# A two-layer vision kernel: the last token groups' routing moved among the second attention's first steps

## The chip, the cores and the metric

The kernel runs on one core of a Trainium2 chip, as one launch. The metric is device time in microseconds. Three runs of the kernel before took 2015.39, 2020.72 and 2024.27 us; the median is 2020.72. A separate execution was profiled; all rows below come from it.

## The reference

The input x is 2 images of 256 channels and 56 x 56 pixels, in float32. Layer 0 normalises groups of channels, makes q, k and v by a 1x1 and a depthwise 3x3 convolution, and lets each pixel attend to a 7x7 neighbourhood: four heads with dilation 1 (branch 0), four with dilation 2 (branch 1). The projected result is added to x. Layer 1 sees the 6272 pixels as tokens of 256 values: a linear attention (one sum of keys and values per image) with a feed-forward part, then a mixture of experts. Cut to what matters here:

```python
x = x + _L0_conv_ref(_gn(x), ...)                 # convolutions, 7x7 neighbourhood attention
t = _to_tokens(x)
t = t + _L1_attn_ref(_ln_t(t), ...)               # linear attention and feed-forward
t = t + _L1_ffn_ref(_ln_t(t), ...)                # 8 experts, the best 2 of each token
# in _L1_ffn_ref
logits = xt @ Wr + br
top_p, top_idx = jax.lax.top_k(softmax(logits), 2)
weights = top_p / top_p.sum(axis=-1, keepdims=True)
h = gelu(einsum('end,edh->enh', layernorm(xt) * ln_g + ln_b, W1) + b1)
y = einsum('enh,ehd->end', h, W2) + b2
```

All of it has to be computed, and the output has the shape of x.

## The kernel before

The program is written as Python generators that are stepped in turn, and a planner (a list scheduler in the compiler) orders each engine's instructions from it. Inside a block marked as a manual schedule, TensorE keeps the order of the program text. The other engines and the DMA queues take the planner's order, which is fixed at compile time; each queue works strictly in order on the chip. Buffers are tiles in pools. A pool that opens on bytes of closed pools makes each of its tiles wait for the last users of the tiles that lay there.

The work runs in these stages. First, image 0: convolutions and neighbourhood attention together (`first_image`). Second, `layer1` begins with image 0's half of the linear layer (`linear`, half 0) while the convolutions of image 1 end. Third, the neighbourhood attention of image 1 (`Attention`, b = 1), with expert tiles of image 0's tokens filled in between its steps. Fourth, image 1's half of the linear layer, also mixed with expert tiles. Last, the rest of the expert tiles and the output.

In half 0 the tokens go in six groups of 512 (four blocks of 128), by `steps` and a table of letters, `parts`: each letter advances one generator by one step. `q` and `m` are queries and messages, `f` is `feed_forward` (four products with a ReLU, `oc` 0 to 3, then the output products two blocks at a time), `r` and `p` are both `route`. `route` has these steps: in the first, TensorE multiplies the router's weights with the tokens (`pa`), an engine copies the product to `la`, VectorE takes the tokens' statistics, GpSimd two powers, and VectorE writes normalised tokens to `row`. In the second, TensorE turns `la` (`pl`), and VectorE finds the best two experts (`top_two`) and counts (`cnt`). In the third, TensorE gives each token its rank among its expert's (`pp`), VectorE makes the indices `si`, and the ACT queue stores the tokens to y2 (`store`). Then come four steps of two scatters each: GpSimd's queue writes 128 rows to `xs` at the indices (L166).

After the last group, `Experts` opens its pools, loads small constants and makes from the counts a table of 17 expert tiles (`full_tiles`, product `pc`, L1356, some 20 small VectorE operations). An expert tile (`Experts.run`) is fetched (`fetch`: rows `xr` from `xs`, weights `w1e` and `w2e`, 1 MB each, all on SP's queue; `so` and `sv`, L1525 and L1529, pick the expert's scales and biases), turned (`turn`, L1538), and multiplied by W1 (L1569) and W2 (L1587), and its result is scattered to y2.

The second attention then opens its own pools. Band by band (8 rows of keys in branch 0), `prepare(g)` loads a group of 448 tokens' q and k in two tiles `ld` (L779, two buffers in all), and four parts of it turn them on TensorE (L747) and copy them out (L756 to L764 and the helper at L180 and L182). `table` loads a band's bias table in eight DMAs (L690, `tab`; in branch 0 two buffers). A score step multiplies keys and queries (L637), takes the exponential on ScalarE (L641), multiplies by the table on VectorE (L642), and multiplies by the values `v` (L651); VectorE adds the result to strips (L815) that GpSimd has cleared (L823). `wpr` holds the projection's weights (L616). Each step of the attention yields; from step 22 on (`LEAD`) one step of the expert tiles follows most of them, and the first expert step is the first tile's `fetch`.

Of the kernel before, what the change touches and what calls it, by code (L numbers as in the profile page):

```python
# [20 lines left out]
P = 128  # L21
# [42 lines left out]
LEAD = 22  # L64
XW = C + 4
# [59 lines left out]
def hybrid_kernel(ctx: ExitStack, tc: tile.TileContext, a: dict, out: bass.AP):  # L125
# [471 lines left out]
    class Attention:  # L597
# [6 lines left out]
        def __init__(self, ctx, b, order, banks=None):  # L604
            self.b, self.banks = b, banks
            kw = {"reuse_waits": "tile"} if banks else {}
            self.pool = {
                k: ctx.enter_context(tc.tile_pool(name=f"p2{k}{b}", bufs=self.POOLS[k], **kw)) for k in order.split()
            }
            self.ps_o = ctx.enter_context(tc.tile_pool(name=f"p2po{b}", bufs=1, space=PSUM, **kw))  # L610
            if banks:
                banks.open(ctx)
            self.ps_s = ctx.enter_context(tc.tile_pool(name=f"p2ps{b}", bufs=1, space=PSUM, **kw))
            bp, op = self.pool["b"], self.pool["x"]
            self.wpr = op.tile([P, 2, C], F32, name="wpr", bufs=1)
            nc.sync.dma_start(self.wpr, a["w_proj_t"].rearrange("(s p) o -> p s o", p=P))  # L616
            self.ones = op.tile([TT, HD], F32, name="ones2", bufs=1)
            nc.vector.memset(self.ones, 1.0)
            self.qT0 = bp.tile([P, HH, WW], F32, name="qT0")

            self.qT1 = bp.tile([P, 2, 2, 28, 28], F32, name="qT1")
            self.kT1 = bp.tile([P, 2, 2, 2, 28, KC], F32, name="kT1")
            self.o0 = op.tile([P, HH, WW], F32, name="o0", bufs=1)
            self.held = {}
# [51 lines left out]
        def table(self, s, r, c):  # L676

            held = self.held
            if held.get(s, (None, None))[0] != r:
                nr, (i0, ni), nw = KR[s], rows_of[s][r], wide[s]  # L680
                t = self.pool["t"].tile(
                    [TT, NH * (KR[s] + 6) * nw], F32, name=f"tab{s}", bufs=2 if self.banks and s == 0 else 1
                )
                t = t[: nr * KC, : NH * ni * nw].rearrange("p (h i j) -> p h i j", h=NH, j=nw)
                urgent = tc.high_priority if self.banks and r == 0 and s == 0 else nullcontext
                for kr in range(nr):

                    f = fp[s][1 if r == 0 and kr < 7 else 2 if r == 2 and kr >= nr - 7 else 0]
                    with urgent():
                        ld = nc.sync.dma_start(  # L690
                            t[kr * KC : (kr + 1) * KC].rearrange("p h i j -> p h (i j)"),
                            bass.AP(
                                f.tensor, f.offset + (i0 + 7 - kr) * nw,
                                [[NH * 21 * nw, KC], [21 * nw, NH], [1, ni * nw]],
                            ),
                        )
                held[s] = (r, t)
                anchors["table"] = ld.ins
            if c is None:
                return held[s][1]  # L700
            o = sum(n for _, n in cols_of[s][:c])
            return held[s][1][:, :, :, o : o + cols_of[s][c][1]]

        def run(self):
# [69 lines left out]
            def prepare(g):  # L774

                lds = []
                for k in range(2):
                    ld = ldp.tile([P, 2, 2 * C], F32, name="ld")[:TT]
                    nc.sync.dma_start(ld, yqk[:, 4 * g + 2 * k : 4 * g + 2 * k + 2, :])  # L779
                    lds.append(ld)  # L780
                if banks is None:
                    pm = ps_s.tile([P, 4, 512], F32, name="s_ps")
                    for k in range(4):
                        turned(lds, k, pm[:, k, :])
                    for k in range(4):
                        settle(g, k, pm[:, k, :])
                    return []

                def part(k):
                    pm = banks()  # L790
                    turned(lds, k, pm)
                    settle(g, k, pm)

                return [(g, lambda k=k: part(k)) for k in range(4)]
# [15 lines left out]
            def blocks(rows):  # L810

                return -(-min(rows, HH) * WW * 3 * C // (T * P))
# [7 lines left out]
            def strip0(j):  # L820
                if j not in strips0:
                    strips0[j] = ac.tile([P, 2, 8, WW], F32, name="acc0")
                    nc.gpsimd.memset(strips0[j], 0.0)  # L823
                return strips0[j]

            def band0(r):
                yield blocks(8 * r + 16)
                yield from prepared(r + 1, 1)
# [103 lines left out]
            def band1(r):  # L932
                if r == 3:
                    anchors["last"] = True
                yield blocks(14 * r + 20)
# [381 lines left out]
    class Experts:  # L1317
# [4 lines left out]
        def __init__(self, ctx, tk):  # L1322
# [4 lines left out]
            self.wp, self.w, self.small = pool("p4w", 1), pool("p4w1", 2), pool("p4s", 2)  # L1327
# [168 lines left out]
        def fetch(self, t, nh, pools):  # L1496
# [28 lines left out]
            nc.gpsimd.tensor_tensor(  # L1525
# [83 lines left out]
    def linear(ph, tk, half, behind=None):  # L1609
# [67 lines left out]
        nc.gpsimd.memset(ones, 1.0)  # L1677

# [198 lines left out]
        def feed_forward(n0, n, m2T, out):  # L1877
# [3 lines left out]
            for oc in range(4):  # L1881
                p1 = ps_h.tile([P, 512], F32, name="p1", tag="h")
# [9 lines left out]
            out.append(lb)  # L1892
# [38 lines left out]
        def top_two(lg, up, lb, scale, row, n):  # L1931


            p = sm.tile([P, 4, E], F32, name="prob")[:, :n]
            iob = iota.unsqueeze(1).to_broadcast([P, n, E])
            nc.vector.tensor_tensor(p, lg, bc(up, E), ALU.mult)
            nc.vector.tensor_tensor(p, p, lb[:, :n], ALU.add)
            nc.vector.tensor_tensor(p, p, bc(scale, E), ALU.mult)
            nc.vector.tensor_tensor(p, p, brb.unsqueeze(1).to_broadcast([P, n, E]), ALU.add)
# [16 lines left out]
        def weights(ms, row, n):  # L1956

            r = sm.tile([P, 4], F32, name="rsum")[:, :n]
# [8 lines left out]
        def route(n0, n, lb):  # L1967

            xT = tk.turned(n0, n)
            pa = ps_a.tile([P, 512], F32, name="pa", tag="a")  # L1970
            for ct in range(2):
                for k in range(n):
                    nc.tensor.matmul(
                        pa[32 * k : 32 * k + 32, :P], wr[:, ct, :], xT[:, ct, k * P : (k + 1) * P],
                        start=(ct == 0), stop=(ct == 1), skip_group_check=True,
                    )
            la = lp.tile([P, P], F32, name="la", bufs=1)
            evac(la[: 32 * n, :], pa[: 32 * n, :P])
# [13 lines left out]
            up = sm.tile([P, 4], F32, name="up1")[:, :n]  # L1992
            nc.vector.tensor_scalar(up, tk.up[:, n0 : n0 + n], 1.0, None, ALU.add)
            if n == 4:
                row = lp.tile([P, 4, XW], F32, name="row")
            else:
                row = wk.tile([P, 2, XW], F32, name="row2", tag="z")[:, :n]
            for k in range(n):
                last = norm(row[:, k, 0:C], t[:, k, :], mv, rs, k)
            with tc.issue_after(last.ins):  # L2000
# [3 lines left out]
            pl = ps_a.tile([P, 4, 32], F32, name="pl", tag="a")  # L2004
            nc.tensor.transpose(
                pl.rearrange("p k e -> p (k e)")[:, : 32 * n], la[: 32 * n, :], ident[: 32 * n, : 32 * n]
            )
            ohs, ms = top_two(pl[:, :n, :E], up, lb, r1, row, n)
# [8 lines left out]
            weights(ms, row, n)  # L2017
            yield
            pp = ps_a.tile([P, 4, E], F32, name="pp", tag="a")
            nc.tensor.matmul(pp[:, :n], tri, m[:, :n], start=True, stop=False)  # L2020
            nc.tensor.matmul(pp[:, :n], ones, before[:, :n], start=False, stop=True)
            slot = sm.tile([P, 4, E], F32, name="slot")[:, :n]
            nc.vector.tensor_tensor(slot, pp[:, :n], ebase.unsqueeze(1).to_broadcast([P, n, E]), ALU.add)
# [53 lines left out]
        def keep():  # L2077
# [8 lines left out]
            wk=wk, ps_h=ps_h, ps_q=ps_q, ps_a=ps_a, ps_k=ps_k,  # L2086
# [23 lines left out]
    def layer1(whole, tk, conv_ctx=None, conv=None, behind=None):  # L2110
# [14 lines left out]
        with ExitStack() as ph:  # L2125
            ln = linear(ph, tk, 0, behind)
            with tc.manual_schedule(engines={mybir.EngineType.PE}):
                for i, _ in enumerate(ln.keys()):
# [9 lines left out]
                    "mfpPPPPfmfrfrff", "fpPPPPffrffrf", "pPPPPrr", "pPPPP",  # L2138
                )
                todo = steps(ln, order[:early1], parts, {"k": conv, "w": merging, "x": prepared})  # L2140
                for part in islice(todo, sum(len(t) for t in parts[:8])):
                    pass
# [5 lines left out]
            for _ in islice(todo, len(parts[8])):  # L2148
                pass
            ex = Experts(whole, tk)  # L2150
            table = ex.full_tiles(ln.ps_a.tile([P, E], F32, name="pc", tag="a"), ln.ones)
            next(table)
            for _ in todo:
                pass
            for _ in table:
                pass

        xc = whole.enter_context(tc.tile_pool(name=f"p4c{run}", bufs=2, side="right", reuse_waits="tile"))
# [9 lines left out]
        if run == 0:  # L2168
            with ExitStack() as ph:
# [4 lines left out]
                att = Attention(ph, 1, "l t k b p v r x ac", bank)  # L2174
                first = True
                with tc.manual_schedule(engines={mybir.EngineType.PE}):
                    for i, what in enumerate(att.run()):
                        if i >= LEAD and (what == "scores" or what == "values" or what == "end"):
# [169 lines left out]
```

## Time and profile before

| what | value |
|---|---|
| median of three runs | 2020.72 us (2015.39 to 2024.27) |
| the profiled execution's own time | 2019.04 us |
| its span, first to last instruction | 2017.3 us |
| mean granted TensorE clock | 0.962 |
| busy: TensorE, weight loads | 1841.5 us (91%), 1309.2 us (65%) |
| busy: VectorE, ScalarE, GpSimd | 1087.7 us (54%), 703.3 us (35%), 608.2 us (30%) |
| chain that ended last | PE 68%, DVE 15%, DMA 8%, ACT 4% |
| DMA | 268.77 MB, mean 133 GB/s |

In the rows PE is TensorE, PEld its weight loads, DVE VectorE, ACT ScalarE, POOL GpSimd and SP the engine that issues most DMAs; SPq is its DMA queue. A row of the stage table gives the stretch in us from the span's start, then the mean of one entry, then busy us and number of instructions of each engine, the granted TensorE clock (1.00 is full), the busy share of the DMA engines and GB/s. A row of the waits reads: engine, tile and line that waited, whom for, us in total, times, longest. A row of the timeline has start, duration, engine, line, operation, result and operands, and in brackets the idle time before it and what ended that.

### The profile page before, as it was taken

To read this page: it belongs to the slowest core of one execution; us is meant where nothing else is said; L and a number is where in the kernel's file an instruction comes from. 1 tells how busy PE (TensorE), PEld (TensorE's weight loads), DVE (VectorE), ACT (ScalarE), POOL (GpSimd) and SP (SyncE) were. 2 spreads that over 40 slices of the span, in tenths; PEclk is the share of its full clock that TensorE was granted. 3 is DMA by queue.
4 is the path that set the end of the run, shared out by engine and by line. 5 is a ranking of instruction groups with operands and counts; after the bars stand their busy time and mean duration, and the time that the engine had idled before them with its cause. 6 is when DMAs were issued, how large, how long until landed. Compare 5 with 4: busy or idle time off the path is not lost.

```text
span 2017.3 us, 27769 instructions
## 1 busy us (share of the span) xinstructions
PE 1841.5 (91%) x9996; PEld 1309.2 (65%) x9996; DVE 1087.7 (54%) x2686; ACT 703.3 (35%) x1323; POOL 608.2 (30%) x688
## 2 busy tenths in 40 slices
PE   6999898978899974899989989999899999999996
PEld 3545354556555642556668765668688888888885
DVE  7978988888887553556556434655431212121121
ACT  2333333334343312454535633323322222322332
POOL 4630230035013343111125411345433333333221
PEclk9999899989899985999999989999999999999998
DMA  4653332340111144764465110114576676767995
GB/s 112 161 136 123 117 113 53 110 145 17 40 43 35 59 117 123 215 167 129 123 180 164 55 55 32 43 58 123 166 233 193 191 198 187 198 189 195 299 276 157
DMA packets 199576, 268.77 MB, mean 133 GB/s; under 512 B 30504, under 2 KB 158038, under 8 KB 199184
## 3 DMA queue, kind: packets, MB, share of 16 engines
q1 hardware_dynamic: 167344, 223.87, 36.7%
q0 software_dynamic: 19728, 27.54, 7.3%
q10 hardware_dynamic: 12352, 15.43, 2.2%
q8 instruction: 83, 1.36, 0.3%
q14 instruction: 69, 0.57, 0.1%
HBM read 200.11 MB, written 70.95 MB: 134 GB/s over the span
## 4 chain that ended last, share of the span: by engine, by line
PE 68%; DVE 15%; DMA 8%; ACT 4%; issue 2%; POOL 2%; SPq 1%; ACTq 0%; DVEq 0%; POOLq 0%
PE py L1587 13%; PE ph L1569 13%; PE p L1885 8%; DVE yc L569 5%; PE po L651 4%; PE py L1901 4%; PE py L519 4%; PE x L1587 2%; DMA y<-yt,idi 2%; PE pm L1855 2%; PE x L1569 2%; PE pc L540 2%; PE s_ps L637 2%; PE kx L307 2%; PE pq L1815 2%
## 5 line engine op out<-in xcount | busy, mean ns | idle before, releaser
L1569 PE MATMUL ph<-xe,w1e 128*128 128x256 f32 (+1 forms) x1448 | 310.7, 370 | 14.6 <-ACT hT L1573 8.2
L1587 PE MATMUL py<-w2e,hT 128*128 128x256 f32 x1392 | 311.3, 379 | 0.0
L1573 ACT ACTIVATE hT<-ph,sv 128x256 f32<-128x256 f32 (+1 forms) x362 | 165.8, 462 | 390.9 <-PE ph L1569 386.0
L1569 PEld LDWEIGHTS ph<-xe,w1e 128*128 128x128 f32 x1448 | 262.0, 191 | 53.8 <-ACT hT L1573 10.4
L1587 PEld LDWEIGHTS py<-w2e,hT 128*128 128x128 f32 x1392 | 260.0, 190 | 33.2 <-issue 0.2
L166 POOL DMA_INDIRECT y<-yt,idi x101 | 162.9, 1613 | 252.0 <-DVE yt L1593 136.4
L569 DVE SCALAR_TENSOR_TENSOR yc<-ypad,w,yc 128x1120 f32<-128x1120 f32 x144 | 202.8, 1412 | 26.4 <-ACT yc L559 24.0
L259 POOL TENSOR_TENSOR rs<-rs,mhalf 128x2 f32<-128x2 f32 (+3 forms) x90 | 72.1, 804 | 297.3 <-DVE rs L258 264.2
L519 PE MATMUL py<-x_sb,wq 128*128 128x448 f32 (+1 forms) x384 | 152.5, 528 | 5.1 <-ACT ypad L525 3.5
L641 ACT ACTIVATE p<-s_ps 112x952 f32<-112x952 f32 (+5 forms) x88 | 102.2, 1161 | 149.6 <-PE s_ps L637 102.1
L642 DVE TENSOR_TENSOR p<-p,tab 112x952 f32<-112x952 f32 (+5 forms) x88 | 122.2, 1392 | 43.5 <-ACT p L641 41.0
L1521 DVE CAST idi<-xr 128x2 int32<-128x2 f32 (+1 forms) x53 | 11.2, 211 | 241.6 <-DMA xr<-xs 241.6
L540 PE MATMUL pc<-ypad,diag 128*128 128x448 f32 x324 | 131.7, 547 | 0.0
L1593 DVE SCALAR_TENSOR_TENSOR yt<-py,eq,yt 128x256 f32<-128x256 f32 x87 | 41.9, 482 | 164.8 <-PE py L1587 164.6
L1551 POOL TENSOR_SCALAR yt<-b2e,eq 128x256 f32<-128x256 f32 x101 | 52.3, 524 | 254.4 <-DMA b2e<-in_L_ffn_b 212.0
L166 POOL DMA_INDIRECT xs<-row,si x98 | 100.1, 1021 | 59.1 <-DVE si L2029 29.8
L519 PEld LDWEIGHTS py<-x_sb,wq 128*128 128x128 f32 x384 | 71.1, 196 | 65.9 <-issue 55.5
L562 DVE SCALAR_TENSOR_TENSOR yc<-ypad,w,yc 128x784 f32<-128x784 f32 x96 | 101.6, 1075 | 4.6 <-ACT yc L559 4.0
L540 PEld LDWEIGHTS pc<-ypad,diag 128*128 128x128 f32 x324 | 59.8, 191 | 52.4 <-issue 48.7
L1885 PE MATMUL p<-m2T,fw 128*128 128x512 f32 (+2 forms) x224 | 93.8, 542 | 0.0
L651 PE MATMUL po<-p,v 98*32 98x170 f32 (+5 forms) x960 | 69.5, 370 | 26.1 <-DVE p L642 11.9
L1885 PE MATMUL p<-xT,fw 128*128 128x512 f32 (+1 forms) x208 | 92.7, 568 | 0.0
(376 smaller groups left out, 2906.7 us busy)
## 6 DMA issues: line engine op xcount, KB each, us to landing
w1e<-in_L_ffn_W SPq DMA_DIRECT2D x53, 1024.0 KB
w2e<-in_L_ffn_W SPq DMA_DIRECT2D x53, 1024.0 KB
yd<-yc SPq DMA_DIRECT2D x24, 784.0 KB
ld<-yd SPq DMA_DIRECT2D x28, 448.0 KB
xr<-xs SPq DMA_DIRECT2D x48, 260.0 KB
b2e<-in_L_ffn_b SPq DMA_DIRECT2D x53, 128.0 KB
t<-td SPq DMA_DIRECT2D x12, 512.0 KB
y<-t ACTq DMA_DIRECT2D x24, 256.0 KB
```

Source lines behind the costliest of these rows:

```text
L166: ins = nc.gpsimd.indirect_dma_start(out=dst[:, :], out_offset=bass.IndirectOffsetOnAxis(ap=index, axis=0), in_=src, in_offset=None, **kw,)
L519: nc.tensor.matmul(py[:, :n, :], self.wq1[:, ct, oc * P : (oc + 1) * P], self.x_sb[:, ct, (q0 + g0) * WW : (q0 + g0 + n) * WW], start=(ct ...
L540: nc.tensor.matmul(pc, diag[:, tap, :], ypad[:, dy : dy + SHARE, dx : dx + WW], start=(tap == 0), stop=(tap == 8),)
L562: nc.vector.scalar_tensor_tensor(yc[:, y0:y1, :], src, w, yc[:, y0:y1, :], ALU.mult, ALU.add)
L569: nc.vector.scalar_tensor_tensor(yc[:, y0:y1, :], src, w, yc[:, y0:y1, :], ALU.mult, ALU.add)
L641: nc.scalar.activation(p[:nk, :, :n], s_ps[:nk, :, :n], AF.Exp)
L642: nc.vector.tensor_tensor(grid(p), grid(p), table[:nk], ALU.mult)
L651: nc.tensor.matmul(dst[hs] if w is None else den[hs], v[:nk, hs] if w is None else w[:nk, :], p[:, h, :, o : o + q.shape[2]], start=first ...
L1569: nc.tensor.matmul(p1, x.w1[:, ct, j * P : (j + 1) * P], x.xe[:, ct, :], start=(ct == 0), stop=(ct == 1),)
L1573: nc.scalar.activation(hT[:, j, :], p1, AF.Gelu, bias=x.sv[:, 4 + j : 5 + j])
L1587: nc.tensor.matmul(py, hT[:, j, h * P : (h + 1) * P], x.w2[:, j, :], start=(j == 0), stop=(j == NJ - 1),)
L1885: nc.tensor.matmul(p1[:, :w], fw1[:, k, oc * P : (oc + 1) * P], rhs, start=(k == 0), stop=(k == 3))
```

## The change

Six edits, all at the border between half 0 of the linear layer and the second attention, save for the third and the last.

First, the routing of the last two groups of half 0 takes its buffers from pools of their own (`late`), with copies of the small constants, on the other side of the memory. Second, of that routing only the first two steps stay before the attention. The third step and the scatters of each of the two groups, and the making of the tile table, are stepped from within the attention, ahead of its steps 4, 6, 12, 14 and 16 (`ENDING`). The pools of the expert tiles' weights and rows open at step 16. Third, the router's products move from `route` into `feed_forward`, in both halves: `pa` and `la` ahead of its first product block, `pl` and the scaling by the tokens' deviation (`up`, `lg`) ahead of its third. Fourth, groups 1 and 2 of the second attention's tokens get four buffers of their own (`spare`). Fifth, the second attention fetches the bias tables of its first two bands at its start, ahead of its tokens, and loads `wpr` at the first band of branch 1. Sixth, `so` (all 53 tiles) and the first two strip memsets of the second attention go from GpSimd to VectorE.

```diff
+ENDING = (4, 6, 12, 14, 16)
...
             self.wpr = op.tile([P, 2, C], F32, name="wpr", bufs=1)
-            nc.sync.dma_start(self.wpr, a["w_proj_t"].rearrange("(s p) o -> p s o", p=P))
+            if not banks:
+                self.load_projection()
...
-                held[s] = (r, t)
-                anchors["table"] = ld.ins
+                held[s] = (r, self.ahead.pop((s, r), None) or self.fetch(s, r))
...
-                    ld = ldp.tile([P, 2, 2 * C], F32, name="ld")[:TT]
+                    ld = (self.spare if self.spare and g in (1, 2) else ldp).tile([P, 2, 2 * C], F32, name="ld")[:TT]
                     nc.sync.dma_start(ld, yqk[:, 4 * g + 2 * k : 4 * g + 2 * k + 2, :])
...
-                    nc.gpsimd.memset(strips0[j], 0.0)
+                    (nc.vector if banks and j < 2 else nc.gpsimd).memset(strips0[j], 0.0)
...
             def band0(r):
                 yield blocks(8 * r + 16)
+                if banks is not None and r == 0:
+                    for k in range(2):
+                        self.ahead[0, k] = self.fetch(0, k)
                 yield from prepared(r + 1, 1)
...
             def band1(r):
...
+                if banks is not None and r == 0:
+                    self.load_projection()
...
             so = self.small.tile([P, 4 + NJ, E], F32, name="so")
-            nc.gpsimd.tensor_tensor(
+            nc.vector.tensor_tensor(
                 so, self.sel, tab.oh[:, k, :].unsqueeze(1).to_broadcast([P, 4 + NJ, E]), ALU.mult
             )
...
+        def late(ctx):
+
+            late_s, late_l = (
+                ctx.enter_context(
+                    tc.tile_pool(name=f"p3{k}{run}{half}z", bufs=2, side="right", reuse_waits="tile")
+                ) for k in "sl"
+            )
+            z = SimpleNamespace(sm=late_s, lp=late_l)
...
+            routing.append(z)
+            ns.ones = z.ones
...
             for oc in range(4):
+                if oc == 0:
+                    pa = ps_a.tile([P, 512], F32, name="pa", tag="a")
+                    for ct in range(2):
+                        for k in range(n):
+                            nc.tensor.matmul(
+                                pa[32 * k : 32 * k + 32, :P], wr[:, ct, :], xT[:, ct, k * P : (k + 1) * P],
+                                start=(ct == 0), stop=(ct == 1), skip_group_check=True,
+                            )
+                    la = lp.tile([P, P], F32, name="la", bufs=1)
+                    evac(la[: 32 * n, :], pa[: 32 * n, :P])
+                if oc == 2:
+                    pl = ps_a.tile([P, 4, 32], F32, name="pl", tag="a")
+                    nc.tensor.transpose(
+                        pl.rearrange("p k e -> p (k e)")[:, : 32 * n], la[: 32 * n, :], ident[: 32 * n, : 32 * n]
+                    )
...
+                    nc.vector.tensor_tensor(lg[:, :n], pl[:, :n, :E], bc(up, E), ALU.mult)
...
-                    "mfpPPPPfmfrfrff", "fpPPPPffrffrf", "pPPPPrr", "pPPPP",
+                    "mfpPPPPfmfrfrff", "fpPPPPffrffrf", "rrpPPPP", "pPPPP",
...
+            late = ExitStack()
+            if run == 0:
+                ln.late(late)
+            with tc.manual_schedule(engines={mybir.EngineType.PE}):
+                for part in islice(todo, len(parts[7]) + 2):
+                    pass
+
+            def ending():
+
+                for k in range(2):
+                    if k:
+                        table = ex.full_tiles(ln.bank()[:, :E], ln.ones)
+                        next(table)
+                    next(todo)
+                    yield
+                    for part in islice(todo, 4):
+                        pass
+                    yield
+                for _ in table:
+                    pass
...
+        def experts():
+
+            late.close()
+            ex.opened()
+            return whole.enter_context(tc.tile_pool(name=f"p4c{run}", bufs=2, side="right", reuse_waits="tile"))
...
+                spare = late.enter_context(tc.tile_pool(name="p2z1", bufs=4, side="right", reuse_waits="tile"))
+                att = Attention(ph, 1, "l t k b p v r x ac", bank, spare)
+                ln.bank = bank
...
                     for i, what in enumerate(att.run()):
+                        if i in ENDING:
+                            next(ending, None)
+                        if i == ENDING[-1]:
+                            xc = experts()
```

## The prediction

> **What bounds the kernel now.** I read the page first: PE is busy 91% of the span and carries 68% of the chain that ended last, so in most places a microsecond saved on another engine is worth nothing. The 40 slices show one hole: PE at 2 tenths and PEclk at 5 in the sixteenth slice (about 756 to 807 us). The busy time by stage puts edges to it.
>
> ```profile
> core 0: us, PE busy (x) PEld busy (x) DVE busy (x) ACT busy (x) POOL busy (x), PEclk, DMA share, GB/s
> ...
> 680.00:739.00 59.00, 59.00 (x242) 35.73 (x241) 29.46 (x146) 15.88 (x45) 28.65 (x31) 1.00 0.27 77
> 739.00:747.00 8.00, 3.65 (x17) 2.77 (x16) 6.82 (x33) 1.43 (x6) 1.42 (x2) 0.91 0.76 166
> 747.00:800.00 53.00, 22.53 (x139) 14.29 (x139) 19.13 (x112) 7.76 (x17) 22.70 (x27) 0.50 0.43 124
> 800.00:820.00 20.00, 12.46 (x121) 6.18 (x118) 11.33 (x24) 6.94 (x10) 1.78 (x3) 0.82 0.95 244
> 820.00:860.00 40.00, 37.01 (x373) 25.57 (x373) 22.18 (x43) 21.78 (x29) 9.75 (x8) 1.00 0.68 181
> ```
>
> PE is full until 739 and nearly full from 820. Between lie 81 us with 38.6 us of PE time, 22.5 of them at half the granted clock: some 27 us of work at full clock. No other engine is full either (DVE 37 us), so the stage is bound by waits in turn. The waits of that stretch name them:
>
> ```profile
> PE x L747 <- DVE qT L764: 13.4, 1, 13.4
> ...
> DVE sv L1529 <- POOL so L1525: 10.8, 1, 10.8
> ...
> PE x L747 <- DMA ld<-yd: 9.4, 4, 3.8
> ...
> PE pc L1356 <- DVE cnt L2016: 5.4, 1, 5.4
> PE pp L2020 <- DVE rsum L1961: 5.2, 1, 5.2
> PE po L651 <- DVE p L642: 4.8, 1, 4.8
> ```
>
> Read as a story: PE waits for the routing of the last two groups (pp, pc), starts the second attention's transposes, and stands 13.4 us because VectorE, next in whose order is a small sum (sv), waits for GpSimd, which works off 16 scatters before it comes to `so`. Then PE waits for token loads, then for the second bias table. The timeline of SP's queue shows why those two come late:
>
> ```profile
> 729.65 6.74 SPq L690 DMA_DIRECT2D tab<-fp  x8
> 736.50 0.47 SPq L779 DMA_DIRECT2D ld<-yd  x1
> 745.46 0.39 SPq L616 DMA_DIRECT2D wpr<-in_w_proj_t  x1
> 745.91 0.46 SPq L779 DMA_DIRECT2D ld<-yd  x1
> 751.12 5.66 SPq L831 DMA_DIRECT2D v<-yd  x8
> 775.86 0.82 SPq L779 DMA_DIRECT2D ld<-yd  x2
> ...
> 785.12 0.81 SPq L779 DMA_DIRECT2D ld<-yd  x2
> ...
> 797.21 4.16 SPq L690 DMA_DIRECT2D tab<-fp  x5
> ...
> 807.25 0.39 SPq L1505 DMA_DIRECT2D xr<-xs  x1
> ```
>
> Two buffers hold one group's tokens, so each pair is sent only when PE has turned the pair before. `wpr` stood 8.4 us in the queue ahead of a token load. The expert tiles' first load (xr) leaves at 807.25.
>
> **The marker.** The first PE instruction of the expert tiles (turn of xr, L1538) runs at 816.8, the first expert product at 819.8. The order of PE's work after it is unchanged and PE is 93% busy there (37.0 of 40 us), so I count the gain as the shift of this point and let it carry to the end.
>
> **What goes, gross.** Routing ahead of the attention: last feed-forward product ends at 742.7, first attention transpose at 759.2: 16.5 us. The wait on qT: 13.4. Token loads on the chain: 5.91 and 5.41, 11.3. Last table pieces: from the issue at 797.2 to DVE's start at 809.5, 12.3. Sum 53.5, an upper end that ignores what is late next.
>
> **What is late next, step by step, with rows of before.** SP first. The first table leaves at 729.7 to 736.4, as now (it waits for a token store). The change fetches the second table at once, ahead of the token loads in program order: 8 x 0.83 (4.16/5) = 6.6, to 743.0. Two token loads at 0.41, and 5.7 to land (mean of 5.91 and 5.41): 749.6. If the planner puts the tokens first: 742.9. I take the late one; the other is kept for the range. Groups 1 and 2 follow in the spare buffers; 0.92 MB at the 218 GB/s of 785 to 790 are 4.2, so group 1 is there by 754.
>
> Then eight parts of four transposes and their copies. Three parts took 3.2 us at half clock (782.2 to 785.4): 8.5, so the first scores at 758.1. PSUM is free: the feed-forward's last reads end near 745.
>
> Then four score steps. 792.30 to 802.35 held three with their transposes, mostly at half clock: 3.35 each, 13.4, to 771.5. Two more at full clock (802.35 to 804.80, 2.45 each) to the point where the expert loads are asked for: 776.4.
>
> That load (xr) needs all scatters. Group 5's counts are done near 757 (757.8 in before; its chain of three `pow` on GpSimd, 743.9 to 750.5, stays). Its rank product stands at step 12 of the attention, about 764; slot to index 1.3 us (759.4 to 760.7); eight scatters at a pitch of 1.26 are 10.1, landing 2.5: 778. Group 4's eight run before, from about 752, since its top-two moves into DVE's idle time at 730 to 737 (it no longer waits for pl at 738.8).
>
> xr lands 4.6 us after issue (807.25 to 811.86), so the turn is at 782.6 and the first product 3.0 to 7 us later (w1e took at most 11.6 us from issue to use): 786 to 790 against 819.8.
>
> Shift 30 to 34; I take **30**, since three queues must all go as counted. The profiled execution took 2019.04 us (span 2017.3), so 1989; the median of the runs shown is 2020.72, 1.7 above it, so **1990**.
>
> **Edits costed at nothing.** `so` on DVE: 53 of 128x96, between DVE's 128x64 product (0.21) and 128x136 (0.29), 0.25 by nearness, 13 us of DVE; from 1500 on DVE is busy 10 of 50 us, in the attention 28 of 50. Uncovered, one per tile on the switch: below 0.3 x 53 = 16 us late, or early by the 0.39 that POOL spends; I take 0. Two strip memsets on DVE: from 0.1 (its 112x32) to 1 each (POOL takes 0.82), once, beside transposes. `wpr` later: one issue of 0.39 before the table of the other branch; needed at 858. Constants loaded twice: five small issues near 643, where SP idles until 729 save for one store. The tile table (some 20 DVE operations, 758.5 to 763.0) moves among score steps, where DVE does 2 of 3 us. Router products in the feed-forward: the same 16 products, copy, transpose and two DVE operations, in other places. DVE waited 14.6 us for pl between 1250 and 1480, but PE had 49 of 50 us there in most slices, so I take 0.
>
> **A rule against it.** Eight scatters took 13.4 us beside the convolution's VectorE work (641.9 to 655.3) and 9.8 beside an idle one (763.6 to 773.4):
>
> ```profile
> 641.93 1.75 POOL L166 DMA_INDIRECT xs<-row,si  x1 [3.94 <-DVE si L2029]
> 643.98 1.69 POOL L166 DMA_INDIRECT xs<-row,si  x1 [0.30 <-DVE yc L562]
> ...
> 766.16 0.96 POOL L166 DMA_INDIRECT xs<-row,si  x1 [0.30 <-issue]
> ```
>
> So the scatters may end at 781.6 instead of 778, which lowers the shift by 3.6. [...]
>
> The granted clock stayed 0.50 while the three parts of 759 to 762 ran, and came back at 800 after some 8 us of scores and values; that is why the transposes and the first four steps are priced at half clock. [...]
>
> **Rivals.** *The wait moves to xr.* On SP everything behind xr (w1e, w2e, the next tokens and v) waits with it. If group 5's index work queues behind table products on VectorE (three steps, 10 us) and scatters run at 1.75, xr leaves near 791 and the shift is 14 to 16: 2005. For: DVE and POOL keep program order by a planner, not by the chip. Against: DVE has idle time.
>
> *More than counted.* Tokens ahead of the second table (6.7 earlier) and a clock that stays up (half of about 12 us of PE in transposes and first steps, 6): shift 42, 1979. Against: the scatters hold it unless GpSimd is early too.
>
> *Slower: PE stands for `la` in the feed-forward.* The router's transpose now sits between the feed-forward's products, at 14 places, and PE waits there until ACT or DVE has copied `la`; the feed-forward's own products are behind it. The cover is two product blocks (3.5 us each). VectorE's waits on POOL reach 4.7 us and ACT's on DVE's top-two 4.6. A wait of a whole block each time costs 14 x 3.6 = 50, less 30: 2040. It decides from 2.1 us a group. Against: in before the distance is one block (709.0 to 713.2) and PE waited 1.3 us for `la`, once.
>
> *It doesn't do what it says.* The attention's tiles lie on the routing's old bytes, and routing still reads late tokens there; if the planner orders the rest of the routing first, the hole stays: 2020.
>
> **Chances.** Forecast (1980 to 2000) 0.52; xr 0.20; more 0.14; la 0.09; unchanged 0.05. The range leaves out the slower cases and the ends: 1975 to 2010. Measurement can tell some 0.5% (10 us) from no change. Faster by more: forecast, more, and 0.16 of xr's 0.20: 0.82. Same: 0.04 + 0.05 = 0.09. Slower 0.09.
>
> **What would show it.** In the profile after: no wait of sv on `so`; PE's first attention transpose near 750, not 759; second table issued right behind the first; six token loads in a row; first turn of xr near 783 and its wait on the scatters; half clock still between 747 and 771. A first turn after 800, or PE waits on `la` in the feed-forward summing to over 10 us, would make the prediction wrong.

## The result and the profile after

The changed kernel took 2042.09 us (median of 4, 2038.92 to 2048.76) against 2021.94 for the kernel before on the same chip; the recorded ratio is 1.0109, 95% interval 1.0074 to 1.0144 (the two medians alone give 1.0100). It is some 1% slower. The forecast was 1990. The profiled execution took 2041.49 us (span 2039.7; 2017.3 before).

The first question is where the time went. For that I took the k-th matmul of the same tiles in both traces and subtracted the times; below, "shift" is that difference, after less before.

| place in before (us) | shift | what lies between |
| --- | --- | --- |
| 545 | +1.6 | |
| 705 | +7.2 | half 0's feed-forward: 5.6 lost |
| 816.8 (first turn of xr) | -12.5 | border: 19.7 gained |
| 856 | -7.3 | 5.2 given back |
| 1441 | +5.3 | half 1, most of it from 1258 on: 12.6 lost |
| 1461 | +22.0 | one jump of 16.7 |
| 1522 | +24.9 | 2.9 more |
| end | +22.4 | last stage: 2.5 regained |

So the border did gain, some 20 us. The gain was lost three times over elsewhere. The busy time by stage, in the stretches that the prediction showed of before:

```profile
core 0: us, PE busy (x) PEld busy (x) DVE busy (x) ACT busy (x) POOL busy (x), PEclk, DMA share, GB/s
680.00:739.00 59.00, 58.10 (x223) 34.39 (x222) 33.63 (x180) 15.73 (x45) 26.58 (x29) 1.00 0.18 60
739.00:747.00 8.00, 8.00 (x31) 5.59 (x30) 1.39 (x6) 1.90 (x6) 5.85 (x7) 1.00 0.91 208
747.00:800.00 53.00, 27.73 (x220) 17.77 (x218) 30.20 (x128) 12.51 (x26) 22.13 (x23) 0.70 0.59 144
800.00:820.00 20.00, 15.26 (x125) 9.36 (x125) 11.41 (x24) 11.13 (x16) 3.20 (x5) 0.86 0.88 270
820.00:860.00 40.00, 33.75 (x325) 22.99 (x322) 19.71 (x38) 15.31 (x19) 6.48 (x7) 0.87 0.65 164
```

PE is full 8 us longer (feed-forward later by 7.2), does 27.7 us instead of 22.5 between 747 and 800, and has a new gap after 820. The waits of the border (739 to 820) name new causes; the wait of sv on `so` is gone:

```profile
...
PE x L757 <- DMA ld<-yd: 18.6, 2, 17.9
POOL xs L167 <- DVE si L2069: 15.5, 1, 15.5
ACT m L2014 <- DVE m L2013: 12.8, 1, 12.8
...
PE po L657 <- DVE p L648: 5.8, 1, 5.8
```

PE now stands once, 17.9 us, for the first tokens; GpSimd stands 15.5 us for the ranks. SP's queue shows why the tokens are late (start, duration):

```profile
736.12 23.68 SPq L704 DMA_DIRECT2D tab<-fp  x16
759.91 0.96 SPq L789 DMA_DIRECT2D ld<-yd  x2
...
797.73 0.38 SPq L1521 DMA_DIRECT2D xr<-xs  x1
```

Sixteen table pieces, both tables, stand ahead of the tokens and take 23.7 us instead of the 13.3 counted. SP's waits between 735 and 765 say what held them:

```profile
SPq L704 <- DMA y<-t: 10.2, 2, 6.9
SPq L704 <- DVE row L154: 3.8, 1, 3.8
```

By these waits the second table's buffer takes over bytes of token tiles `t` of half 0, which the stores `y<-t` read. Its last six pieces waited for the last group's stores, sent at 748.59 and 752.12. And the jump of 16.7 us near 1461 is one wait (PE, 1440 to 1490, then SP, 1440 to 1480):

```profile
PE px L1554 <- DMA xr<-xs: 14.2, 1, 14.2
PE ph L1585 <- DMA w1e<-in_L_ffn_W: 2.6, 1, 2.6
```

```profile
SPq L1521 <- DMA xs<-row,si: 57.4, 1, 57.4
```

14.2 + 2.6 = 16.8, about the jump. (The lower clock behind the stall adds some 3 us, see the last section; against that stand, by the rows of PE, some 3 us of router products and small waits that only before has in this stretch.) SP stood 57.4 us for a scatter before it could send xr, with w1e behind it, sent at 1469.79, 0.9 us after xr; PE did 1.65 us of work between 1457 and 1474, and its granted clock there was 0.62. In before, xr loads left at 1436.09 and 1454.35, ahead of the last scatters, which ran from 1456.63 to 1465.02. SP's queue, first the changed kernel, then before:

```profile
1468.87 0.34 SPq L1521 DMA_DIRECT2D xr<-xs  x1
1469.79 0.38 SPq L1525 DMA_DIRECT2D w1e<-in_L_ffn_W  x1
```

```profile
1436.09 0.35 SPq L1505 DMA_DIRECT2D xr<-xs  x1
...
1454.35 0.35 SPq L1505 DMA_DIRECT2D xr<-xs  x1
```

**Theory.** Three separate causes. (1) *Layout*: the new tile `lg` (128 bytes, three buffers) makes half 1's small pool end at 25552 instead of 25168. The last stage's first xr buffer begins at 25280. It now lies on the index tiles `si`, which the last scatters read, and so waits for them. (2) *Router products* in the feed-forward cost time there. (3) *The border* gained less than forecast, because SP's, ScalarE's and VectorE's orders held the attention's start. **Rival** to (1): the jump comes from the router products' places on PE.

### The profile page after: what moved, and what is told of

The parts are those of the page before. It is cut to its first block, busy times and chain, and to the rows that moved or that the text cites. A ratio compares the mean times of both kernels' runs of the same rounds, so it can differ in the third digit from the quotient of the medians.

```text
span 2039.7 us, 27727 instructions
## 1 busy us (share of the span) xinstructions
PE 1843.3 (90%) x9996; PEld 1310.0 (64%) x9996; DVE 1090.3 (53%) x2741; ACT 698.6 (34%) x1321; POOL 585.4 (29%) x634
## 4 chain that ended last, share of the span: by engine, by line
PE 45%; DMA 5%; DVE 4%; ACT 3%; POOL 1%; issue 1%; SPq 0%; ACTq 0%; DVEq 0%; POOLq 0%
PE ph L1585 13%; PE py L1603 13%; PE p L1939 3%; PE x L1603 2%; PE py L1955 2%; DMA y<-yt,idi 2%; PE x L1585 2%; PE po L657 2%; DMA xs<-in_c_fill 1%; PE kx L308 1%; PE kp L296 1%; PE s_ps L643 1%; PE px L1554 1%; PE x L348 1%; DMA xr<-xs 1%
## 5 line engine op out<-in xcount | busy, mean ns | idle before, releaser
L1537 DVE CAST idi<-xr 128x2 int32<-128x2 f32 (+1 forms) x53 | 11.3, 214 | 237.6 <-DMA xr<-xs 237.6
L657 PE MATMUL po<-p,v 98*32 98x170 f32 (+5 forms) x960 | 69.8, 372 | 33.8 <-issue 16.7
```

The source lines that it names most:

```text
L657: nc.tensor.matmul(dst[hs] if w is None else den[hs], v[:nk, hs] if w is None else w[:nk, :], p[:, h, :, o : o + q.shape[2]], start=first ...
```

## Experiments

Ratios are to runs of the kernel before on the same chip, with 95% intervals; 0.001 is 2.0 us. Shifts are of single profiled executions; some of these were already up to 7 us apart from before at 545, ahead of any edit, so times of two runs near 750 to 800 compare to a few us only.

### Layout: e1 and e2

e1 is the changed kernel with `lg` in another pool, which puts the last stage's bytes back:

```diff
-                    lg = sm.tile([P, 4, E], F32, name="lg")
+                    lg = lp.tile([P, 4, E], F32, name="lg", bufs=3)
```

> The changed kernel with one edit: the new logits tile lg (3 x 128 bytes) comes from the pool of the routing's rows (lp) instead of half 1's small pool (sm), so that the small pool ends at byte 25168 again and the last stage's first xr buffer (from 25280) no longer lies on the last groups' index tiles. Theory (layout): the wait of 14 us on xr near 1458, the w1e wait behind it and the fall of the clock go: 17 us (16.7 is the jump of the shift at 1441 to 1461) below the changed kernel's 2042, so 2025, within 4; no long PE wait between 1440 and 1480. Rival (feed-forward): the jump comes from the router products' new places on PE, which this edit leaves alone: 2042, and the wait on xr stays.

Measured: 1.0028 (1.0008 to 1.0048), 16 us below the changed kernel's ratio. No PE wait between 1440 and 1490 is over 1.4 us.

e2 is the kernel before with one tile of the same pool made larger by as many bytes. The same work is computed:

```diff
-            lb = sm.tile([P, 4, E], F32, name="lb")
+            lb = sm.tile([P, 8, E], F32, name="lb")[:, :4]
```

> The kernel before with one edit: the tile lb in the small pool is taken twice as large (256 instead of 128 bytes, 3 buffers, so 384 bytes more); no instruction is added or removed. Theory (layout): the last stage's first xr now lies on the index tiles of the last groups as in the changed kernel and waits for their scatters: 17 us slower, 2038, within 5, with a PE wait on xr of over 8 us near 1450. Rival (feed-forward): 2022, no such wait.

Measured: 1.0103 (1.0079 to 1.0127), 21 us slower. PE's waits in 1440 to 1480, then SP's:

```profile
PE px L1538 <- DMA xr<-xs: 9.8, 1, 9.8
PE pp L2020 <- DVE chosen L2011: 3.3, 1, 3.3
```

```profile
SPq L1505 <- DMA xs<-row,si: 48.0, 1, 48.0
```

384 unused bytes alone make the old kernel as slow as the changed one, by the same wait of SP for a scatter; in e1 that wait is gone. The layout theory holds, the rival falls.

### Router products: e3, e4, e7, e10, e11

e3 leaves the products in the feed-forward only for the two groups whose routing moved into the attention; elsewhere they are in `route` as before (and `lg` no longer grows half 1's pool):

```diff
+            lg, here = None, run == 0 and half == 0 and (n0, n) in order[early1 - 2 : early1]
             for oc in range(4):
-                if oc == 0:
+                if oc == 0 and here:
```

> The changed kernel with the router products in the feed-forward only for the last two groups of the first half (those that are routed among the attention); all other groups have them in the routing as before, and half 1's small pool is back at its old size. Theory (layout, and a feed-forward that pays for the router products): 17 us for the layout, some 12 us for half 1's feed-forward (the shift grew by that from 1258 to 1421) and up to 5 for half 0's: 2042 - 17 - 14 = 2011, within 5. If the feed-forward's share was something else (only the layout counts): 2025. Rival (the border itself lost): 2030 or more.

Measured: 0.9951 (0.9937 to 0.9966), 10 us faster than before. Against e1 (1.0028) the products of the other groups cost 15.6 us. (Its profiled execution, 2004.22, was the shortest of its runs, up to 2014.69, so I read waits from it, not sums.)

e4 is the kernel before with the products moved for all groups; `lg` lies in the pool of the rows, which grows by 384 bytes:

```diff
             for oc in range(4):
+                if oc == 0:
+                    pa = ps_a.tile([P, 512], F32, name="pa", tag="a")
...
+                if oc == 2:
+                    pl = ps_a.tile([P, 4, 32], F32, name="pl", tag="a")
...
+                    lg = lp.tile([P, 4, E], F32, name="lg", bufs=3)
...
```

> The kernel before with one part of the change alone: the router products of all groups moved into the feed-forward, with lg in the pool of the rows, so that the small pool and the last stage's addresses stay as before. Theory (the feed-forward pays): 5.5 us in half 0 and 12 in half 1, so 2022 + 17 = 2039 at most; 2032 if half of it is due to the shifted border. Rival (the products are free there, as the prediction had it): 2022.

Measured: 1.0065 (1.0041 to 1.0090), 13 us slower. PE never waited for `la` in it, and yet it lost time. One place shows how (VectorE; the first fence is e4, the second before):

```profile
644.26 3.17 DVE L562 SCALAR_TENSOR_TENSOR yc<-ypad,w,yc 128x784 f32<-128x784 f32 x3
647.35 0.68 DVE L182 COPY m2T<-mts 128x512 f32<-128x512 f32 x1
```

```profile
641.63 3.17 DVE L562 SCALAR_TENSOR_TENSOR yc<-ypad,w,yc 128x784 f32<-128x784 f32 x3
644.72 0.69 DVE L182 COPY m2T<-mts 128x512 f32<-128x512 f32 x1
```

With the logits ready early, the planner put a group's top-two on VectorE (640.9 to 643.4) ahead of three convolution operations, and these ahead of the copy `m2T`, for which PE's product `pd` waits. PE stood 1.93 us for it, and some 3 us were lost in all (the shift goes from +0.6 before it to +3.5 after it). The same wait stands near 1378 in half 1. It isn't the whole cost: of the 17 us by which the shift of e4 grows between 1240 and 1522, 7.2 arise after 1500 (4.0 in e10 below). There xr loads leave later, and SP waited 21.6 us for fills of `xs` between 1478 and 1530, 6.6 in before.

One rival is left. e4, and e10 and e11 below, also make the pool of the rows larger by 384 bytes, and no run makes it larger alone. None of the waits on `xs<-row,si` that mark e2 stands in e4 or e10, but that these bytes cost nothing is argued, not shown.

e7 is e3 with the products moved for all groups of half 0; e10 and e11 are the kernel before with them in half 1 or half 0 alone (in each, the condition `here` is `half == 0` or `half == 1`).

> The run with router products for the late groups only, with the products in the feed-forward for all groups of half 0 and none of half 1. Theory (half 1 is where they cost, half 0's loss is swallowed by the wait at the border): 2012, same as with the late groups only, and 12 to 14 us under the run with all groups. Rival (half 0 costs its 4 to 5 us to the end): 2017.

> The kernel before with the router products in the feed-forward of half 1 alone (lg in the pool of the rows). Reading A (the shifts of the run with both halves, which grew by 16 us between 1330 and 1540): 2035. Reading B (the ratios of the three runs on the changed kernel: 12 us for half 0, 3.5 for half 1): 2025.

> The kernel before with the router products in the feed-forward of half 0 alone. Reading A (the 4.7 us lost in half 0 were gone at 775, swallowed by the border's waits): 2022. Reading B (12 us, as on the changed kernel): 2033.

Measured: e7 1.0011 (0.9996 to 1.0026); e10 1.0072 (1.0045 to 1.0100); e11 1.0015 (0.9998 to 1.0032). On the kernel before, reading A holds: half 1 pays it all (14.5 us), and half 0's loss is gone at the border. On the changed border my expectation for e7 missed: there half 0's four groups cost 12 us to the end, and half 1 only 3.4 (e1 less e7, give or take 5). Why the split differs is not settled: a wait at the border that swallows half 0's loss is one candidate, the planner's other orders are another. In the one profiled execution of each, e7 gains 11.4 us between 705 and the first turn of xr and e3 18.5, so on the changed border the loss isn't swallowed; it grows. The sum, 13 to 16 us, agrees on both kernels.

### The border: e5, e6, e9

e5 is e3 with the second table asked for after the tokens:

```diff
-                    for k in range(2):
-                        self.ahead[0, k] = self.fetch(0, k)
+                    self.ahead[0, 0] = self.fetch(0, 0)
                 yield from prepared(r + 1, 1)
+                if banks is not None and r == 0:
+                    self.ahead[0, 1] = self.fetch(0, 1)
```

> The run before with router products for the late groups only (ratio 0.9951, some 2012), with one edit: the second bias table is no longer asked for before the tokens of the third group are, so that its pieces, which wait for the feed-forward's last token stores (7.4 us there), no longer stand ahead of token loads on SP's queue. Theory (SP's order set the start of the attention): the first transposes move from 759.3 to 743 to 750, the marker (first turn of xr, 797.9) by 8 to 10, so 2003. Rival (the scatters and xr hold the marker wherever the tokens are): 2009 or more.

Measured: 0.9934 (0.9912 to 0.9957), 3.4 us under e3, with intervals that overlap. (The profiled execution, 1999.56, was the shortest of its runs, up to 2014.43.) The tokens came: the first transposes ran at 744.4, 15 us earlier, 2.7 of them a lead that this execution had at 742 already. But PE then stood 11.1 us for ScalarE's copies of them, so the size came out nearer the rival's (2007.23 in the median), by another wait. e6 adds earlier ranks:

```diff
-ENDING = (4, 6, 12, 14, 16)
+ENDING = (0, 2, 10, 12, 16)
```

> The run with the second table later, and the routing's parts spread earlier among the attention's steps: (0, 2, 10, 12, 16) instead of (4, 6, 12, 14, 16), so that the rank product of the last group but one does not stand behind transposes that wait for tokens (GpSimd idled 14.5 us ahead of its scatters). Theory: xr leaves 5 to 10 us earlier and the 5.7 us that PE waits for VectorE behind xr go: 1998. Rival (the marker is bound by PE's steps ahead of it, not by xr): 2003, as without this edit.

Measured: 0.9915 (0.9894 to 0.9935). Against e5 the intervals overlap. xr left at 784.05 (789.12 in e5, 791.29 in e3), yet the first turn did not come earlier (795.5, 794.8 in e5): the rival's case. What held PE is on ScalarE (e6):

```profile
757.46 0.20 ACT L2020 ACTIVATE m<-m 128x4 f32<-128x4 f32 x1 [11.93 <-DVE m L2019]
757.57 0.53 ACT L766 ACTIVATE qT<-x 128x448 f32<-128x448 f32 x1
```

The first attention copy (qT) is queued behind the Exp of the last group's weights, which waited 11.9 us for VectorE's top-two. PE had turned the tokens at 746.6 and stood 8.39 us. So e9 issues the last group's top-two after the copies of the first two token groups:

```diff
-                    "mfpPPPPfmfrfrff", "fpPPPPffrffrf", "rrpPPPP", "pPPPP",
+                    "mfpPPPPfmfrfrff", "fpPPPPffrffrf", "rpPPPPr", "pPPPP",
...
+                            anchors["settled"] = nc.vector.tensor_scalar(
...
+                    if not k:
+                        with tc.issue_after(anchors["settled"]) if run == 0 else nullcontext():
+                            next(todo)
+                        yield
```

with ENDING = (0, 4, 8, 12, 14, 16), so the other parts of the routing move by some steps too.

> The run with the ranks earlier (ratio 0.9915, some 2005), where PE started its transposes at 746.6 and then stood 8.4 us behind the Exp of the last group's weights, which stands ahead of the transposes' copies on ScalarE (and the last group's top-two ahead of them on VectorE). Edit: the last group's top-two is issued after the copies of the first two token groups. Theory (the routing's order on ScalarE and VectorE is what is late next): first scores at 757 instead of 765.3, the marker (first turn of xr, 795.5) at 787 to 789; 1998. Rival (xr is bound by the last group's counts, which now come later): the marker stays at 795, 2005.

Measured: 1993.16 us, ratio 0.9868 (0.9842 to 0.9893): 27 us under the kernel before, the fastest of all. The busy time by stage and the marker on PE (e9):

```profile
680.00:739.00 59.00, 59.00 (x250) 34.54 (x249) 33.89 (x177) 15.12 (x44) 27.37 (x30) 1.00 0.21 69
...
747.00:800.00 53.00, 39.37 (x274) 22.88 (x278) 33.38 (x136) 16.30 (x30) 23.27 (x25) 0.65 0.74 207
800.00:820.00 20.00, 17.78 (x180) 12.94 (x176) 11.64 (x19) 9.94 (x11) 4.05 (x4) 1.00 0.49 143
```

```profile
747.50 0.39 PE L757 MATMUL x<-ident,ld 112*128 112x112 f32 x2
749.14 2.05 PE L757 MATMUL x<-ident,ld 112*128 112x112 f32 x10 [1.25 <-DMA ld<-yd]
756.12 1.73 PE L757 MATMUL x<-ident,ld 112*128 112x112 f32 x8 [4.93 <-DVE qT L774]
...
787.11 0.63 PE L1555 MATMUL x<-ident,xr 128*128 128x128 f32 x4 [0.39 <-DMA xr<-xs]
```

PE works 39.4 us of the 53 (22.5 in before, 27.7 in the changed kernel). The first turn is at 787.1, and PE and xr arrive there almost together: PE waits 0.39 us for xr. The shift is -29.7 at this turn; PE then stands 3.8 us for w1e at 792.1, the shift is -24.9 at 856, and that much holds to the end (-25.8).

### Two edits costed by the prediction: e8 and e12

e8 is e3 with `so` back on GpSimd; e12 is e6 without the spare token buffers:

```diff
-            nc.vector.tensor_tensor(
+            nc.gpsimd.tensor_tensor(
...
```

```diff
-                    ld = (self.spare if self.spare and g in (1, 2) else ldp).tile([P, 2, 2 * C], F32, name="ld")[:TT]
+                    ld = ldp.tile([P, 2, 2 * C], F32, name="ld")[:TT]
```

> The run with router products for the late groups only, with so back on GpSimd. Theory (as the prediction had it, so on VectorE costs and brings nothing away from the border; at the border GpSimd now works the scatters of two groups until 796 and so would stand behind some of them): 2012 if it is hidden, up to 2020 if VectorE waits for it at the border (10.8 us was that wait before).

> The run with the ranks earlier, without the spare token buffers: each pair of token loads waits again until PE has turned the pair before. Theory (as the prediction counted them): token loads come back on the chain, 5.4 to 11.3 us slower: 2010 to 2016. Rival (hidden, since the last group's routing holds the transposes' copies meanwhile): 2005.

Measured: e8 0.9960 (0.9946 to 0.9974) against 0.9951, no difference that the intervals can tell, though VectorE stood 5.8 us ahead of `sv` at the border of e8. e12 0.9959 (0.9940 to 0.9978) against 0.9915: 8.9 us, and PE's waits for token loads come back (10.9 us in five waits, 735 to 830).

## Why the prediction was wrong

- **"Router products in the feed-forward ... I take 0"** is the first failed step, and it failed twice. As work order it costs 13 to 16 us (e4; e1 against e3; the bytes of the pool of the rows, in these runs too, were not tried alone). As memory it costs some 16 us (e1) to 21 us (e2): the tile `lg` was not weighed at all, since I counted instructions and waits of the moved products, not the bytes of the new tile. Without these two the changed kernel gains 10 us (e3).
- **The rival on `la`** (2040, chance 0.09) gave the time (2042 measured) by luck, with the wrong mechanism. It asked for PE waits on `la`; there were none. The cost came through VectorE's and ScalarE's order and through bytes.
- **"8 x 0.83 = 6.6 ... 749.6"**, the tokens. The pieces do cost 0.8 each, but the second table's buffer waits for token stores of the last group. I had this kind of wait for the first table and did not ask it for the second. Tokens were used at 767.0: 7.2 late from the feed-forward, 10.2 from this.
- **"Eight parts ... 8.5; four steps 13.4"**: the rows of 782.2 to 785.4 held fourteen transposes, three and a half parts, so eight parts at that pace are 7.4. Right in size all the same: 9.2 from the first transpose to the first scores (776.21), 13.2 for four steps (789.44). The next two took 6.3 instead of 4.9. Half clock did stay over them (0.50 between 760 and 772).
- **"Group 4's eight run ... from about 752"**: wrong. The rank product is in PE's written order behind transposes that wait for tokens, so GpSimd stood 15.5 us and the scatters began at 773.67. xr left at 797.73, not 778, the first turn was at 804.28, not 782.6. Of these 21.7 us, 7.2 are from the feed-forward, 10.2 from the tokens and 4.3 from the rest. The turn is past 800, which the prediction had named as a sign that it is wrong.
- **The rival "The wait moves to xr"** (a shift of 14 to 16, chance 0.20) is near the border's own size (-12.5 at the turn), but its reason is not the one at work: the index work stood behind transposes that waited for tokens, not behind table products, and the scatters did not run at 1.75.
- **Not seen**: the next late thing behind the tokens, ScalarE's Exp and VectorE's top-two of the last group ahead of the first copies (e5, e6, e9). "Group 5's counts are done near 757" was right (757.1 in e3; 763.9 in the changed kernel, whose feed-forward ends later), and I did not ask what is queued behind them.
- **"Gain carries to the end"**: not from the first turn of xr. In the changed kernel 5.2 us went back by 856, where VectorE stood 9.5 us for a later xr with the attention's sums behind it. In e9, too, 4.8 us go back by 856; only from there does the gain carry (-24.9 at 856, -25.8 at the end).
- **Right**: `so` on VectorE at 0 (e8), spare buffers worth 5.4 to 11.3 (8.9 in e12), and, in size, the border's worth: it is 27 us in e9, where 30 was forecast. But e9 has other orders on SP, PE, ScalarE and VectorE than the prediction described, so that the sizes agree is in part luck. `wpr` later, the memsets and the second set of constants were not tried alone.

The slower scatters that I had weighed against the change hardly showed. The 16 scatters beside table products took 22.6 us from 773.67 to 796.25, against 19.9 at their idle pace (0.96 each, 0.30 between two), with one wait of 1.25 for VectorE among them; their own times exceed 0.96 by 1.7 us in all. The longest took 1.49 us, where three of the eight beside the convolution in before took 1.69 to 1.75. In e3 one of the 16 took 1.75.

## What to carry to other kernels

Where pools are reused by bytes, a new tile has a second price: ask which later tile now lies on which earlier one, and when that one's last reader runs. When work moves earlier, list on every engine what is queued behind it; a small operation that waits can hold up much more (in e6 an Exp of 0.2 us waited 11.9 us with the first copies behind it, and PE stood 8.39 us). And when a change made of several parts loses, try its parts alone: here the core, with its orders mended, was worth 27 us, and two effects of one side edit (the bytes of `lg`, 16 us, and the place of the router products, 16 us) together cost more than that.

## What was not expected of the hardware

After the stall of PE at 1457 to 1471 the granted clock was 0.78 over 1474 to 1491, where before had 1.00 over the matching 1450 to 1467 and e1, without the stall, 1.00 over 1474 to 1491. The first 16 products of 128x256 behind it took 6.70 us; 22 of the same size had taken 4.91 us just ahead of it, at which pace 16 are 3.6. So this stall of 14.2 us cost, by estimate, some 3 us more after it had ended. The rows of the clock (the changed kernel, then before) and of PE:

```profile
1474.00:1491.00 17.00, 15.32 (x60) 12.96 (x61) 7.77 (x39) 4.97 (x9) 1.87 (x4) 0.78 0.90 318
```

```profile
1450.00:1467.00 17.00, 15.75 (x80) 12.82 (x80) 15.21 (x93) 7.73 (x13) 10.17 (x10) 1.00 0.62 178
```

```profile
1451.83 4.91 PE L1603 MATMUL py<-w2e,hT 128*128 128x256 f32 x22
...
1475.42 6.70 PE L1585 MATMUL ph<-xe,w1e 128*128 128x256 f32 x16 [2.62 <-DMA w1e<-in_L_ffn_W]
```

Runs of one program also spread widely: e3's eleven lie between 2004.22 and 2014.69, e12's between 2006.26 and 2024.02.
